# Counting image 0's key ranks by triangles, with TensorE adding the other half

## The chip, the cores and the metric

The program runs on one core of a Trainium2 chip. A core has five engines with a queue of their own: TensorE (PE; its weight loads are listed as PEld), VectorE (DVE), ScalarE (ACT), GpSimd (POOL) and SyncE (SP), which here only issues transfers. Each queue is worked off in order; engines wait for each other by semaphores. The metric is device time in microseconds (us); lower is better.

## The reference, cut to what matters

The input x has 2 images of 256 channels and 64 x 64 places, so N = 4096 places an image. Two layers follow each other.

```python
# layer 0: a sparse attention
e = prelu(batchnorm(conv3x3(x)))                 # 64 channels
sim = e^T e ; p = sparsemax(sim)                 # rows of 4096
x = x @ p + x
# layer 1: a pairwise layer with a relu of a sum
a   = w_t . theta(x)      # one number a place
bsc = w_p . phi(x)        # one number a place, the "key"
f = relu(a[n] + bsc[m] + wf_b) / N
y = f @ g(x)              # y[n] = sum over m with key[m] > -a[n] of (a[n] + key[m]) * g[m] / N
x = batchnorm(wz @ y) + x
```

Layer 1 needs no 4096 x 4096 matrix: if the places m are sorted by their key, then y[n] is taken from running sums of g[m] and key[m] * g[m] up to the position of -a[n] in the sorted keys. Sorting means that each place must learn its rank: the number of places whose key is larger, with ties broken by index.

## The kernel before, in words

Both images stay in SBUF. Layer 0 (lines 341 to 863) makes e by convolution, surveys e^T e for the few rows whose sparsemax is not just the place itself, recomputes up to 3 x 128 such rows (`rows`, 12 units of 1024 columns), and multiplies them into x (`attend`: 16 blocks an image of 3 matmuls of 128x512, each added to x by VectorE after GpSimd multiplied that stretch of x by a mask). Layer 1 starts with `project` (image 0) or `project_in` (image 1): for each tile of 128 places g, the key and a.

The class `Ranked` (lines 980 to 1257) does layer 1 by sorting. Image 0 does it with all R = 32 tiles of keys; image 1 with R = 16 tiles, while its other 16 tiles are multiplied out directly by `pair_f` (ScalarE writes relu(a + key) for 128 x 1024 pairs) and `pair_py` (TensorE, 64 steps of two matmuls). The steps for an image are:

- `keys` (line 994): the keys are made fit to be compared; `spread` sends them through DRAM and brings them back as one row in all partitions (`kb`, 128 x R*128).
- `above` (line 1027), once a tile t of 128 places: each partition compares its own key with all R*128 keys and adds the results up, as two instructions, the columns before tile t and those from it on. On VectorE it is a comparison with 0 or 1 as result (line 1041); on ScalarE a sign with -1 or 1 (line 1036), which is halved later. The comparison results go to `junk` and are not read; only the sums (`cnt`) count. The planner picks the engine of each tile.
- `ties` (line 1052): equal keys within a tile, on VectorE.
- `place` (line 1060), every 4 tiles: the sums become ranks.
- `scatter` (line 1072): GpSimd writes each tile's rows of g and keys into a DRAM table `sg` at their ranks.
- `load`, `products`, `sums`, `before`, `raised`, `stored` (lines 1086 to 1122): the sorted table is read back, summed up, and stored as `tb`. `load` needs all scatters of its image. For image 0 it overwrites the place of `kb` and of `ga_0`.
- `segments`, `places`, `counts` (1132 to 1157): find for each a its position; `fetch` (1159): GpSimd gathers the rows of `tb`; `taken` and `finish` (948, 1169): scale, turn, multiply by wz, add to x, send out.

All instructions are put on their queues by a planner (`Plan`, line 94). Each task has a cost for every engine that can do it, a rank (smaller goes first among tasks that are not late), tasks that it comes after, and `Ring` holds that stand for the buffers of a pool (`ring_sim` for the 3 PSUM tiles of `ps_sim`). The planner takes the tasks by its own estimates of time, so that a change of costs, ranks or tasks moves instructions on every queue. The ranks are the constants of line 281 (`A1` for image 1's attention, `K0` and `K1` for the counts, `PY` for the pair products and so on).

Two lines of `begin` (1215 and 1219) make the counts of an image:

```python
u = plan.task({"D": 0.25 + 0.00107 * n, "A": 0.66 + 0.00083 * n}, lambda e, t=t: self.above(t, e == "A"), r, [sp, *room])
places += [u, plan.task({"D": 0.36}, lambda t=t: self.ties(t), r + 0.02, [sp, *room])]
```

Of the kernel before, what the change touches and what calls it, by code (L numbers as in the profile page):

```python
# [8 lines left out]
F32 = mybir.dt.float32  # L9
# [10 lines left out]
P = 128  # L20
# [170 lines left out]
def sparse_path(ctx: ExitStack, tc, a, out, rows_i):  # L191
# [89 lines left out]
    DB, CV1, LS, RW0, SV1, RW1, A0, G0, A1, R0, K0, CH0, R1, K1, CH1, P1, P2, SP1, PY, PF = -16.17, 6.58, -12.34, -22.91, -12.37, -25.58, 4.52, -11.7, -8.57, -12.21, -3.49, 3.38, 7.24, 3.51, 6.34, -23.46, 1.78, 11.05, 19.06, -27.14  # L281
# [698 lines left out]
    class Ranked:  # L980
# [8 lines left out]
        def __init__(self, b, ga, R, at):  # L989
            self.b, self.ga, self.R, self.at, self.junk = b, ga, R, at, None  # L990
            self.key = None if ga is None else ga[:, 0:R, CI + 1]
            self.on_act = []
# [34 lines left out]
        def above(self, t, on_act):  # L1027

            self.made()
            kb, cnt = self.kb, self.cnt  # L1030
            n = self.R * P
            for d, (c0, c1) in enumerate(((0, t * P), (t * P, n))):
                if c0 == c1:
                    continue
                if on_act:
                    nc.scalar.activation(  # L1036
                        self.junk[:, 0, c0:c1], kb[:, c0:c1], AF.Sign, scale=STEEP,
                        bias=self.bound[:, d, t : t + 1], accum_out=cnt[:, t, 3 + d : 4 + d],
                    )
                else:  # L1040
                    nc.vector.tensor_scalar(  # L1041
                        self.junk[:, 1, c0:c1], kb[:, c0:c1], self.key[:, t : t + 1], None,
                        (ALU.is_ge, ALU.is_gt)[d], ALU.add, accum_out=cnt[:, t, d : d + 1],
# [4 lines left out]
        def made(self):  # L1048
            if self.junk is None:
                self.junk = self.at("junk", [P, 2, self.R * P], BF16)  # L1050

        def ties(self, t):

            self.made()
            nc.vector.scalar_tensor_tensor(  # L1055
                self.junk[:, 1, ts(t, P)], self.kb[:, ts(t, P)], self.key[:, t : t + 1], low,
# [3 lines left out]
        def place(self, t0):  # L1060

            b = self.b
            for t in range(t0, t0 + 4):
                if t in self.on_act:
                    nc.vector.memset(self.cnt[:, t, 0:1], float(self.R * P // 2))
# [3 lines left out]
            nc.vector.tensor_reduce(rk[:, 1], cnt[:, :, 3:5], AX.X, ALU.add)  # L1069
            nc.vector.scalar_tensor_tensor(self.rank[:, ds(t0, 4)], rk[:, 1], 0.5, rk[:, 0], ALU.mult, ALU.add)  # L1070
# [133 lines left out]
        def begin(self, rank, after, ranked, chained, then, room):  # L1204
# [7 lines left out]
            self.places_done, self.ranked, places = [], [], []  # L1212
            for t in range(self.R):
# [654 lines left out]
```

## Time and profile before

| | us |
|---|---|
| median of 3 runs | 702.23 (701.17 to 708.35) |
| the profiled execution | 735.76 |
| its span, first to last instruction | 734.0 |
| TensorE busy | 610.9 |
| VectorE busy | 538.9 |
| ScalarE busy | 380.4 |
| GpSimd busy | 209.0 |
| counts on ScalarE, line 1036 | 96.8 in 52 instructions |
| counts on VectorE, line 1041 | 75.5 in 42 instructions |
| scatters, line 1076 | 47.2 in 48 instructions |
| pair products, line 1437 | 127.5 in 256 records |

All durations come from one profiled execution, which took longer than the median of the others; the place of a step is given in us from the start of its span. A float32 matmul appears as two records, so that 256 records of line 1437 are 128 matmuls. A row of the timeline gives the start, the duration, the engine, the line, the operation, the tiles written and read, and in brackets how long the engine was idle before and what ended that.

### The profile page before, as it was taken

How to read it: one execution, taken by the hardware profiler on the slowest of the kernel's cores; microseconds unless marked ns; L12 is line 12 of the kernel's file. 1: busy time of each engine (PE TensorE's matmuls, PEld its weight loads, DVE VectorE, ACT ScalarE, POOL GpSimd, SP SyncE). 2: the span in 40 equal slices, each digit the busy share in tenths (PEclk: the TensorE clock that was granted, in tenths of full speed). 3: DMA queues.
4: the chain of work that ended last, by engine and by line, in shares of the span. 5: the costliest groups of instructions: out<-in, count | busy, mean ns of one | idle time of the engine just before them, and what ended most of it. 6: DMA issues, size and time to landing. Idle time of an engine off the chain costs nothing.

```text
span 734.0 us, 7973 instructions
## 1 busy us (share of the span) xinstructions
PE 610.9 (83%) x2629; PEld 295.4 (40%) x2629; DVE 538.9 (73%) x1052; ACT 380.4 (52%) x534; POOL 209.0 (28%) x274
## 2 busy tenths in 40 slices
PE   5998999999778699999895767759979986971993
PEld 4664444444332233434542223554445543430441
DVE  6876877877879878677759999977988835661404
ACT  0123575666458474764047999979934411400340
POOL 0118920000030311102020675440520176175300
PEclk9998999999889899999988888969989767997898
DMA  9621000101210000000113000127133534474304
GB/s 350 202 58 30 1 15 15 29 1 29 87 28 0 1 0 1 0 1 1 58 28 145 7 29 18 34 87 207 37 90 101 240 104 131 174 235 129 108 1 149
DMA packets 32824, 54.42 MB, mean 74 GB/s; under 512 B 12786, under 2 KB 19812, under 8 KB 31876
## 3 DMA queue, kind: packets, MB, share of 16 engines
q1 hardware_dynamic: 27252, 40.60, 16.5%
q0 software_dynamic: 5088, 12.61, 6.3%
q10 hardware_dynamic: 432, 0.59, 0.3%
q8 instruction: 23, 0.38, 0.2%
q14 instruction: 29, 0.24, 0.1%
HBM read 31.62 MB, written 20.07 MB: 70 GB/s over the span
## 4 chain that ended last, share of the span: by engine, by line
PE 54%; DVE 25%; issue 6%; DMA 5%; another core or an unknown queue 4%; ACT 3%; POOL 2%; SPq 0%; DVEq 0%; ACTq 0%; POOLq 0%
PE sv L476 15%; PE av L836 8%; DVE junk L1041 8%; PE py L1437 7%; PE cv_out L363 6%; PE cv_in L363 6%; PE g L873 2%; DVE junk L1055 2%; PE pz L960 2%; DMA kb<-rd_k 2%; PE sv L508 2%; PE pk L1145 2%; DVE mq L777 2%; POOL r L1162 2%
## 5 line engine op out<-in xcount | busy, mean ns | idle before, releaser
L528 ACT ACTIVATE sv<-sv,nthr 128x1024 f32<-128x1024 f32 (+1 forms) x133 | 131.2, 986 | 96.7 <-PE sv L508 48.9
L524 DVE TENSOR_TENSOR xbs<-sv,xbs 128x1024 f32<-128x1024 f32 (+1 forms) x120 | 130.7, 1089 | 38.4 <-PE sv L476 31.3
L476 PE MATMUL sv<-e 64*128 64x512 f32 x512 | 135.4, 641 | 2.3 <-DVE lim L534 1.2
L836 PE MATMUL av<-z,xbs 128*128 128x512 f32 x192 | 106.9, 693 | 30.2 <-DVE x L843 16.1
L1437 PE MATMUL py<-f,ga 128*128 128x512 f32 x256 | 127.5, 649 | 0.0
L1429 ACT ACTIVATE f<-ab,ga 128x1024 f32<-128x1024 f32 x64 | 71.6, 1142 | 103.9 <-issue 59.9
L1036 ACT ACTIVATE junk<-kb,bound 128x1536 bf16<-128x1536 f32 (+26 forms) x52 | 96.8, 1861 | 5.8 <-DMA kb<-rd_k 5.2
L1162 POOL DMA_INDIRECT r<-tb,k x64 | 61.6, 962 | 81.4 <-DVE tab L1109 38.4
L1041 DVE TENSOR_SCALAR_CACHE_REDUCE junk<-kb,ga 128x1664 bf16<-128x1664 f32 (+20 forms) x42 | 75.5, 1834 | 2.6 <-DMA kb<-rd_k 2.1
L836 PEld LDWEIGHTS av<-z,xbs 128*128 128x128 f32 x192 | 38.1, 215 | 94.3 <-issue 61.7
L476 PEld LDWEIGHTS sv<-e 64*128 64x128 f32 x512 | 45.7, 195 | 68.6 <-issue 43.7
L1437 PEld LDWEIGHTS py<-f,ga 128*128 128x128 f32 x256 | 51.3, 209 | 54.1 <-issue 52.3
L1076 POOL DMA_INDIRECT sg<-ga,rank x48 | 47.2, 984 | 70.1 <-DVE rank L1070 52.1
L964 DVE SCALAR_TENSOR_TENSOR x<-pz,s,x 128x512 f32<-128x512 f32 x32 | 23.0, 746 | 60.1 <-PE pz L960 28.6
L363 PE MATMUL cv_out<-v,wu 128*64 128x256 f32 (+1 forms) x384 | 49.6, 398 | 7.5 <-DVE v L325 7.5
L363 PE MATMUL cv_in<-v,wu 128*64 128x256 f32 (+1 forms) x384 | 46.6, 382 | 1.0 <-ACT c L374 1.0
L446 POOL TENSOR_TENSOR sq<-es 128x512 f32<-128x512 f32 x8 | 8.9, 1106 | 134.3 <-ACT es L437 111.9
L363 PEld LDWEIGHTS cv_out<-v,wu 128*64 128x64 f32 x384 | 28.9, 142 | 31.5 <-issue 14.2
L1182 PE MATMUL yr<-ident,r 128*128 128x128 f32 x64 | 14.0, 307 | 29.9 <-DVE r L1175 16.1
L960 PE MATMUL pz<-yT,wz_sb 128*128 128x512 f32 x64 | 33.5, 664 | 4.7 <-DVE yT L1189 2.1
L363 PEld LDWEIGHTS cv_in<-v,wu 128*64 128x64 f32 x384 | 27.9, 136 | 21.6 <-issue 10.1
L831 POOL TENSOR_TENSOR x<-x,mask 128x1024 f32<-128x1024 f32 x16 | 34.4, 2153 | 0.0
(207 smaller groups left out, 749.4 us busy)
## 6 DMA issues: line engine op xcount, KB each, us to landing
out<-x SPq DMA_DIRECT2D x32, 256.0 KB
tb<-tab SPq DMA_DIRECT2D x3, 2056.0 KB
x<-in_x SPq DMA_DIRECT2D x8, 512.0 KB
tab<-sg SPq DMA_DIRECT2D x3, 1040.0 KB
x<-in_x SPq DMA_DIRECT2D x4, 544.0 KB
e<-e SPq DMA_DIRECT2D x16, 128.0 KB
et<-es SPq DMA_DIRECT2D x16, 128.0 KB
mask<-kd SPq DMA_DIRECT2D x2, 1024.0 KB
```

What stands on the lines that cost most here:

```text
L363: nc.tensor.matmul(d[jp, g][ts(h, CR), n, (r0 - r) * HH : (r1 - r) * HH], lhsT=taps(j, kc, dy), rhs=v[:, kc, r0 + dy - 1 : r1 + dy - 1], s ...
L476: nc.tensor.matmul(ps[:, ts(h, CB)], lhsT=lhs(h), rhs=e[ts(h, CR), q], start=True, stop=True)
L524: nc.vector.tensor_tensor(out=acc[:, cols], in0=d[i, q][:, cols], in1=acc[:, cols], op=ALU.max)
L528: nc.scalar.activation(ps, ps, AF.Relu, bias=both["nthr"][:, i : i + 1], accum_out=got_s["over"][:, i, q : q + 1])
L836: nc.tensor.matmul(pss[j, ct], lhsT=got["xb"][:, k, ts(ct, P)], rhs=got["zs"][k][:, ts(j, CB)], start=(k == 0), stop=(k == KB - 1),)
L960: nc.tensor.matmul(d["z"][:, ct], lhsT=wz_sb[:, ts(ct, P)], rhs=d["y"], start=True, stop=True)
L1036: nc.scalar.activation(self.junk[:, 0, c0:c1], kb[:, c0:c1], AF.Sign, scale=STEEP, bias=self.bound[:, d, t : t + 1], accum_out=cnt[:, t, 3 ...
L1041: nc.vector.tensor_scalar(self.junk[:, 1, c0:c1], kb[:, c0:c1], self.key[:, t : t + 1], None, (ALU.is_ge, ALU.is_gt)[d], ALU.add, accum_ou ...
L1076: rows = nc.gpsimd.indirect_dma_start(out=self.sg, out_offset=bass.IndirectOffsetOnAxis(ap=self.rank[:, t : t + 1], axis=0), in_=self.ga[: ...
L1162: nc.gpsimd.indirect_dma_start(out=self.r[:, t % TH], out_offset=None, in_=self.tb, in_offset=bass.IndirectOffsetOnAxis(ap=self.k[:, t : t ...
L1429: nc.scalar.activation(fm, am, AF.Relu, bias=bm)
L1437: nc.tensor.matmul(pys[q][:, ts(h, CB)], lhsT=ga1[0][:, m, 0:CI], rhs=f[0][:, m % 4, ts(h, CB)], start=(m == NR), stop=(m == NT - 1),)
```

## The change

For image 0 (R = NT = 32, `folded`), `above` compares tile t only with the columns from tile t on. The results are 0 or 1 (VectorE) or -1 or 1 (ScalarE), kept as bf16 in one of four slots (two tiles, `junk` in room S3 and `junk2` in S5, two halves each). For every later tile u, the column sums of what tile t wrote tell how many of t's keys are smaller than each key of u; 128 minus that is what u would have counted against t. `below` adds these column sums up on TensorE: stationary is a column of ones (or of halves for a tile from ScalarE), moving are up to 512 columns of the slot, and the result is one row of PSUM, at partition 0, 32, 64 or 96, and in bank 0 or 1, for each 512 keys. The sums stay in one `ps_sim` tile; a product with zeros opens and closes each bank. After tile 14 the first 16 tiles' sums are complete, after tile 30 the others'. Then `below_out` copies each row of 512 to SBUF, `below_turned` turns it into columns by four matmuls with a stationary row and -1, and `place` adds it, with the known constant, to the tile's own count. So image 0 is placed after tile 15 and after tile 31, not every 4 tiles. Image 1 (R = 16) counts as before. `ties` writes to a tile of its own. Image 0's counts also come after the last products of image 1's `rows`, whose e lies in S5, and `pair_rest`, which writes to S5, comes after the counts. The planner's ranks on line 281 are changed, and a rank BE for the new tasks is added.

```diff
-    DB, CV1, LS, RW0, SV1, RW1, A0, G0, A1, R0, K0, CH0, R1, K1, CH1, P1, P2, SP1, PY, PF = -16.17, 6.58, -12.34, -22.91, -12.37, -25.58, 4.52, -11.7, -8.57, -12.21, -3.49, 3.38, 7.24, 3.51, 6.34, -23.46, 1.78, 11.05, 19.06, -27.14
+    DB, CV1, LS, RW0, SV1, RW1, A0, G0, A1, R0, K0, CH0, R1, K1, CH1, P1, P2, SP1, PY, PF, BE = 6.71, 6.58, -12.34, -12.34, -12.37, -12.64, -10.46, -11.7, -4.84, -15.38, 3.21, 3.33, -11.7, 3.51, 6.41, 4.08, -11.87, -6.07, 12.61, -11.87, -4.72
...
+            self.slots, self.ring, self.folded = [], Ring(4 if R == NT else 2), R == NT
...
+        def slot(self, i):
+            if not self.slots:
+                for name in ("junk", "junk2")[: self.ring.n // 2]:
+                    junk = self.at(name, [P, 2, self.R * P], BF16)
+                    self.slots += [junk[:, 0], junk[:, 1]]
+            return self.slots[i % self.ring.n]
+
+        def above(self, t, on_act, d):
+            slot = d["slot"] = self.slot(self.used if self.folded else int(on_act))
+            self.used += 1
+            kb, cnt, n = self.kb, self.cnt, self.R * P
+            d["on_act"] = on_act
+            for k, (c0, c1) in enumerate(((0, t * P), (t * P, n))):
+                if c0 == c1 or (self.folded and k == 0):
                     continue
...
+        def below(self, t, d):
+            def zeros(h, **flags):
+                nc.tensor.matmul(
+                    self.sums_of[:, h], lhsT=part_ones[:, 2:3].to_broadcast((P, P)), rhs=d["slot"][:, N - CB : N], **flags
+                )
+            if t == 0:
+                self.sums_of = ps_sim.tile([P, CT, CB], F32, name=f"below_{self.b}", tag="sim")
+                for h in range(CT):
+                    zeros(h, start=True, stop=False)
+            for q in range((t + 1) // 4, self.R // 4):
+                c0, c1 = max((t + 1) * P, q * CB), (q + 1) * CB
+                p = 32 * (q % 4)
+                nc.tensor.matmul(
+                    self.sums_of[p : p + 1, q // 4, c0 - q * CB : CB], lhsT=part_ones[:, ds(int(d["on_act"]), 1)],
+                    rhs=d["slot"][:, c0:c1], start=False, stop=False,
+                )
+            if t % 16 == 14:
+                zeros(t // 16, start=False, stop=True)
+
+        def below_out(self, q, d, e):
+            p = 32 * (q % 4)
+            row = d["row"] = work.tile([P, CB], F32, name=f"below_{self.b}_{q}", tag="wa")
+            (nc.scalar.copy if e == "A" else nc.vector.tensor_copy)(row[p : p + 1], self.sums_of[p : p + 1, q // 4])
+
+        def below_turned(self, q, d):
+            p = 32 * (q % 4)
+            d["bt"] = ps_av.tile([P, 4], F32, name=f"bt_{self.b}_{q}", tag="av")
+            for k in range(4):
+                nc.tensor.matmul(
+                    d["bt"][:, k : k + 1], lhsT=d["row"][p : p + 1, ts(k, P)], rhs=minus[p : p + 1, 0:1],
+                    start=True, stop=True,
+                )
...
+        def place(self, t0, bt):
...
+                if self.folded:
+                    known = t * P - sum(u in self.on_act for u in range(t)) * (P // 2)
+                    known += (R - t) * P // 2 if t in self.on_act else 0
...
+                if not last:
+                    v = plan.task(
+                        {"P": 0.15 + 0.1 * (self.R // 4 - (t + 1) // 4)}, lambda t=t, d=d: self.below(t, d), BE, [u] + below[:1],
+                        take=None if t else hb, free=[hj],
+                    )
...
+                if t % 16 == 14:
+                    for q in range(q - 3, q + 1):
+                        hr, ho, d = ring_y.hold(), ring_av.hold(), {}
+                        waiting.append((q, d, ho))
+                        v = plan.task(
+                            {"D": 0.6, "A": 0.65}, lambda e, q=q, d=d: self.below_out(q, d, e), ranked - 0.7, list(below),
+                            take=hr, free=[hb] if 4 * q + 4 == self.R else [],
+                        )
+                        self.ranked.append(v)
+                        d["turned"] = plan.task({"P": 0.6}, lambda q=q, d=d: self.below_turned(q, d), BE, [v], take=ho, free=[hr])
+                if t % 16 == 15:
+                    for q, d, ho in waiting:
+                        placed(q, places[q] + [d["turned"]], d, [ho])
...
-        {"kb": "S0", "tab0": "S0", "tab1": "S6", "r": "S0", "junk": "S3"},
+        {"kb": "S0", "tab0": "S0", "tab1": "S6", "r": "S0", "junk": "S3", "junk2": "S5"},
...
-    r0.begin(R0, [turn0], K0, CH0, {"ab": a_of_0, "rest": None}, conv1)
+    r0.begin(R0, [turn0], K0, CH0, {"ab": a_of_0, "rest": None}, [*conv1, *rw1])
...
-        rest_tasks.append(plan.task({"A": 0.95}, lambda q=q: pair_rest(q), PF - 1, [u], free=[hq]))
+        rest_tasks.append(plan.task({"A": 0.95}, lambda q=q: pair_rest(q), PF - 1, [u, *r0.ranked], free=[hq]))
```

## The prediction

> **What bounds the kernel now.** I read the granted clock and span first (734.0 us in the span, 735.76 us for the execution, clock 0.906), then the chain that ended last, then busy time by stretches of 20 us, then the timeline of each engine from 370 us on. TensorE is the busiest engine, and VectorE's counting lines head what is left of the chain. The stretches show where:
>
> ```profile
> PE 610.9 (83%) x2629; PEld 295.4 (40%) x2629; DVE 538.9 (73%) x1052; ACT 380.4 (52%) x534; POOL 209.0 (28%) x274
> ...
> 420.00:440.00 20.00, 13.13 (x26) 5.24 (x25) 19.82 (x36) 19.84 (x21) 14.76 (x23) 0.83 0.10 33
> 440.00:460.00 20.00, 15.57 (x32) 6.54 (x31) 18.58 (x34) 19.84 (x19) 10.19 (x16) 0.83 0.06 20
> ...
> 500.00:520.00 20.00, 19.22 (x46) 8.67 (x47) 18.17 (x47) 20.00 (x27) 4.21 (x8) 1.00 0.53 142
> ```
>
> In a row the columns are the stretch, then the busy time of PE, PEld, DVE, ACT and POOL. From 400 to 490 us VectorE and ScalarE are full, and TensorE idles a third: this is image 0's count, into which image 1's attention is woven. From 500 us on TensorE is full too. The landmarks I measure by, from the timelines:
>
> ```profile
> 399.40 3.71 ACT L1036 ACTIVATE junk<-kb,bound 128x4096 bf16<-128x4096 f32 x1 [3.97 <-DMA kb<-rd_k]
> 404.15 0.39 ACT L1036 ACTIVATE junk<-kb,bound 128x128 bf16<-128x128 f32 x1
> 404.53 3.59 ACT L1036 ACTIVATE junk<-kb,bound 128x3968 bf16<-128x3968 f32 x1
> ...
> 402.90 0.48 DVE L1041 TENSOR_SCALAR_CACHE_REDUCE junk<-kb,ga 128x256 bf16<-128x256 f32 x1
> 403.30 4.21 DVE L1041 TENSOR_SCALAR_CACHE_REDUCE junk<-kb,ga 128x3840 bf16<-128x3840 f32 x1
> ...
> 464.46 8.23 PE L899 MATMUL g<-gw_sb,x 128*128 128x131 f32 x72
> 489.72 0.39 PE L924 MATMUL pt_k<-ident,ga 128*16 128x128 f32 x1 [4.75 <-DVE bound L1008]
> 494.76 1.88 PE L1437 MATMUL py<-f,ga 128*128 128x512 f32 x4
> ...
> 492.53 0.97 POOL L1076 DMA_INDIRECT sg<-ga,rank  x1 [0.22 <-issue]
> 498.09 2.60 SPq L1091 DMA_DIRECT2D tab<-sg  x2
> 535.48 0.48 DVE L1136 TENSOR_SCALAR oh<-ab,lims 128x512 f32<-128x512 f32 x1
> 583.85 0.98 POOL L1162 DMA_INDIRECT r<-tb,k  x1 [38.42 <-DVE tab L1109]
> ```
>
> So image 0's last scatter starts at 492.5, its table is loaded from 498.1, image 1's keys are turned at 489.7, the pair products (py) start at 494.8, image 0's segments at 535.5, and the fetches at 583.9. After 599 us the records hold two gaps with no visible releaser:
>
> ```profile
> 599.26 11.52 another core or an unknown queue
> 663.48 14.65 another core or an unknown queue
> ```
>
> They make 26 of the 33 us by which this execution exceeds the median of 702.23. I treat them as not part of the ordinary runs, make the sum against the profiled execution as differences, and carry the difference over to the median.
>
> **What the Trainium skill says.** "TensorEngine Tiling (Array Packing)", Key Properties: column tiles work independently, so weight loads and matmuls of different tiles run in parallel, and changing the tiling mode drains the array. The trace agrees on the first: convolution matmuls on two 64-column tiles have a mean record of 382 to 399 ns, yet 24 records take 2.74 us in the chain, 114 ns each. "TensorE: Matmul & The Clock Gate", Back-to-back issue gap: one bf16 matmul of 512 columns takes about 216 ns warm and 427 cold. No such matmul is in this trace; its float32 ones, two records each, take 0.86 us warm (py, 3.45 us for 8 records). "SBUF — State Buffer", Who interferes with whom: a VectorE instruction with two SBUF inputs is held off by a GpSimd instruction that reads SBUF. The trace agrees: the tie instruction (L1055), 0.35 us alone, took 1.66, 1.91 and 2.21 us beside the mask products (2.15 us).
>
> **The change, part by part.**
>
> *Removed.* Image 0's 32 counts of 4096 columns become counts of 128 to 4096, 67,584 columns in place of 131,072. From start to start, ScalarE's cost is 0.33 us + 0.84 ns a column and VectorE's 0.13 us + 1.04 ns (from the five rows above). A full tile cost 4.09 us in its two parts on ScalarE and 4.53 on VectorE. In the built order ScalarE keeps 20 tiles with 44,800 columns, 6.6 + 37.6 = 44 us for about 82; VectorE 12 tiles with 22,784, 1.6 + 23.7 = 25 us for 54. That frees 38 and 29 us in a stretch that both engines fill. It is not what the end gains, because of what follows.
>
> *Added on TensorE.* 136 row sums (8 a tile for tiles 0 to 2, 7 for the next four, down to one), 4 zero products and 32 products of one column. The sums cycle over four 32-column tiles. If all four overlap, the bound is about 0.05 us each; warm in series it is 0.22, cold in series 0.43. I take 0.12: like the convolution's pairs. The upper end costs 93 x 0.31 = 29 us where it counts, see below. Below nothing is excluded: nothing is removed from TensorE.
>
> *A wait added.* There are four junk slots, and a count can start only when TensorE has summed the tile four before it. TensorE's queue is in order, and the built order is: first attention blocks among sums 0 to 5, then nine attention blocks in a row (1_2_0 to 1_6_0), then sum 6. So the counters run four tiles ahead and stop. Estimate: count 0 starts at 395.4 (ScalarE's copy of the key row stands earlier in its queue, before the copies that held it until 390.6); sum 5 is done at about 416; nine blocks x 3 x 0.87 us end at 439.5. ScalarE ends tile 9 at about 419 and then idles 20 us. Queued behind the waiting count is nothing but further counts, but VectorE's place, which image 0's scatters wait for, is behind them. From 439.5: 84 sums x 0.12 = 10, nine attention matmuls 7.8, 16 one-column products 1.5, and 3 of waits on the counters, which run one tile ahead: the first projection (g) at 462, beside 464.5 now. The other half of the freed time goes here.
>
> *Then it pays.* Now VectorE is behind with counts until 488, so projections stand half finished and the keys are late. After: four projection groups x 3.1 us, 9 sums, 16 one-column products and waits, 16 us, and the keys of image 1 are turned at 478.4, 11.3 us earlier. Its key row lands at about 486.5 (8.1 us later, as now), and py starts at about 479, 15 us earlier (ring of the product PSUM: one of three tiles is held by the sums until then; two are enough for the projections, since each is read out within 1 us).
>
> *Moved on GpSimd.* Tiles are now ranked in two batches of 16. The first rank needs count 15, sum 14, a row copy (0.6) and a turn: about 454.5. Then 32 scatters x 1.27 us = 41 us without a pause, so the last ends at 495.3, where it is 493.5 now: scatters started at 418.4 and were spread under the counting. SyncE's table load goes from 498.1 to about 500; behind it in SyncE's queue wait the last key row and image 1's last block of a, needed late. So image 0's table is not earlier. What moves is the work that VectorE had before it: count 1 starts 11 us earlier, so segments start at about 521 (535.5 now). A count tile and six ties (5 us) now lie inside the segments and sums, which leaves the raised table 10 us earlier (557 for 567.3), and the fetches start at about 573.5.
>
> *Small terms.* Row copies (8 x 0.6), the extra memsets and the ties' own tile cost under 5 us on VectorE, inside its slack of 416 to 440. The new rest-after-counts wait is met 30 us before its use. Before 377 us both kernels issue nearly the same order; I take zero.
>
> **Sum.** The fetch path moves by -10, the TensorE path by -15. In the ordinary runs, without the two gaps, TensorE is nearly full from 494 on (about 188 us busy to 724), so its start counts for more than the fetch path: -12 us. The profiled execution would be near 724, the median 702.2 - 12 = **690 us**.
>
> **Rivals.** (1) *Scatters bind* (chance 0.24): the table arrives at 500 to 503, the products wait there 6 us on VectorE with counts queued behind, and the fetch path gains only 3 to 5 us: 698. For it: 41 us of scatters after a first rank at 454; against: TensorE has py to fill in. (2) *Sums in series* (0.12): they don't overlap, and clock gaps while TensorE waits for counters make them cold (granted clock was 0.50 to 0.59 just after idle in this stretch). From 0.25 us a sum, 93 x 0.13 = 12 us, the gain is gone; at 0.43 the counters, ranks and scatters end 29 us later and the time is 719, slower. Against: the convolution's overlap. (3) *The stall is shorter* (0.20): the attention blocks run faster, ranks start near 445, and both paths move by 20: 682. My forecast of 685 to 695 has 0.44. That the sums don't do what they say is no rival: each comparison not made is implied by one made.
>
> **Numbers.** The range is 679 to 704: it takes in rivals 1 and 3, and of rival 2 the part under 0.27 us a sum. Within 1%, 695.2 to 709.3, is about what a measurement can't tell from no change. Faster 0.64 (forecast and rival 3), same 0.24 (rival 1), slower 0.12 (rival 2).
>
> **What would show it.** Right: ScalarE idle about 20 us between counts 9 and 10; g at about 462; keys turned near 478; py near 479; first scatter near 454 and scatters without a pause to 495; table load at 500; segments near 521; a sum every 0.1 to 0.15 us. Wrong: a sum every 0.25 us or more; no idle time in the counts; a scatter end after 500; or a TensorE that idles over 20 us after 500 because f or the fetches come late.

## The result

Beside each other on one chip, the kernel before takes 703.28 us and the kernel after 699.66 us (medians of 20 runs each); the ratio is 0.9936, with an interval of 0.9914 to 0.9957. A second comparison gave 703.47 and 698.48 us, with the same ratio (0.991 to 0.9962). So the change gains 3.6 to 5.0 us. The forecast was 12.

The profiled execution of the kernel after took 699.12 us, with a span of 697.4. Its page and its busy time by stretches, for the rows shown of the kernel before:

```profile
PE 619.3 (89%) x2833; PEld 297.5 (43%) x2833; DVE 523.8 (75%) x1047; ACT 344.5 (49%) x502; POOL 210.8 (30%) x274
...
420.00:440.00 20.00, 16.64 (x38) 6.47 (x36) 19.39 (x53) 0.00 (x0) 6.80 (x7) 1.00 0.00 1
440.00:460.00 20.00, 19.23 (x107) 7.90 (x108) 17.05 (x28) 13.07 (x13) 2.27 (x3) 1.00 0.00 0
500.00:520.00 20.00, 19.94 (x44) 8.79 (x45) 18.06 (x53) 19.31 (x30) 6.75 (x11) 0.91 0.65 179
```

The order of the columns is that of the prediction's rows. ScalarE (the fourth busy column), full from 400 to 490 us in the kernel before, does nothing at all from 420 to 440. VectorE has as much to do as it had, although it counts far less. The wait behind this and the landmarks, from the list of waits and the timelines:

```profile
ACT junk L1051 <- PE below L1079: 37.5, 5, 27.3
```

```profile
392.98 3.75 ACT L1051 ACTIVATE junk<-kb,bound 128x4096 bf16<-128x4096 f32 x1
...
446.93 2.64 ACT L1051 ACTIVATE junk<-kb,bound 128x2816 bf16<-128x2816 f32 x1 [27.28 <-PE below L1079]
...
460.02 1.07 POOL L1136 DMA_INDIRECT sg<-ga,rank  x1 [17.75 <-DVE rank L1127]
...
469.61 2.96 PE L899 MATMUL g<-gw_sb,x 128*128 128x131 f32 x24
...
488.65 0.27 PE L924 MATMUL pt_k<-ident,ga 128*16 128x128 f32 x1
...
488.86 1.88 PE L1535 MATMUL py<-f,ga 128*128 128x512 f32 x4
...
496.90 2.00 ACT L1051 ACTIVATE junk<-kb,bound 128x2048 bf16<-128x2048 f32 x1 [2.79 <-DMA kb<-rd_k]
...
503.08 2.41 SPq L1151 DMA_DIRECT2D tab<-sg  x2
...
524.75 0.48 DVE L1196 TENSOR_SCALAR oh<-ab,lims 128x512 f32<-128x512 f32 x1
...
576.05 1.03 POOL L1222 DMA_INDIRECT r<-tb,k  x1 [34.19 <-DVE kf L1216]
```

Image 0's counts start at 393.0 (395.4 was forecast), ScalarE waits 27.3 us for a row sum (20), the first scatter starts at 460.0 (454.5), the first projection of image 1 at 469.6 (462), image 1's keys are turned at 488.65 (478.4), py starts at 488.9 (479), image 1's key row has landed at 496.9, when its first count starts (486.5), the table is loaded from 503.1 (500), the segments start at 524.75 (521) and the fetches at 576.05 (573.5). Image 0's table, segments and fetches came 3 to 4 us later than forecast. What concerns image 1 came 8 to 10 us late.

The profile of before that the prediction shows stems from an execution of 735.76 us. A clean one (703.56 us, span 701.8) is used from here on; its first projection of image 1, py, first count of image 1 and segments:

```profile
462.73 8.23 PE L899 MATMUL g<-gw_sb,x 128*128 128x131 f32 x72
493.03 1.88 PE L1437 MATMUL py<-f,ga 128*128 128x512 f32 x4
497.57 2.00 ACT L1036 ACTIVATE junk<-kb,bound 128x2048 bf16<-128x2048 f32 x1 [2.73 <-DMA kb<-rd_k]
535.17 0.48 DVE L1136 TENSOR_SCALAR oh<-ab,lims 128x512 f32<-128x512 f32 x1
```

### The profile page after: what moved, and what is told of

It reads as the page before. It is cut to its first block, busy times and chain, and to the rows that moved or that the text cites. A ratio compares the mean times of both kernels' runs of the same rounds, so it can differ in the third digit from the quotient of the medians.

```text
span 697.4 us, 8373 instructions
## 1 busy us (share of the span) xinstructions
PE 619.3 (89%) x2833; PEld 297.5 (43%) x2833; DVE 523.8 (75%) x1047; ACT 344.5 (49%) x502; POOL 210.8 (30%) x274
## 4 chain that ended last, share of the span: by engine, by line
PE 55%; DVE 28%; DMA 7%; issue 5%; POOL 3%; ACT 1%; SPq 0%; DVEq 0%; ACTq 0%; POOLq 0%
PE sv L476 16%; PE av L836 8%; PE cv_out L363 6%; PE cv_in L363 6%; PE py L1535 5%; DVE junk L1056 4%; DVE mq L777 4%; DMA r<-tb,k 3%; DVE tied L1104 3%; PE pz L960 2%; PE g L873 2%; DVE xbs L524 2%; DVE tab L1176 2%; PE sv L508 2%; DVE tab L1169 2%
## 5 line engine op out<-in xcount | busy, mean ns | idle before, releaser
L524 DVE TENSOR_TENSOR xbs<-sv,xbs 128x1024 f32<-128x1024 f32 (+1 forms) x120 | 130.7, 1089 | 37.6 <-PE sv L476 30.5
L1535 PE MATMUL py<-f,ga 128*128 128x512 f32 x256 | 119.0, 613 | 0.0
L836 PE MATMUL av<-z,xbs 128*128 128x512 f32 x192 | 104.4, 671 | 9.8 <-DVE x L843 5.0
L1051 ACT ACTIVATE junk<-kb,bound 128x1792 bf16<-128x1792 f32 (+22 forms) x35 | 60.9, 1747 | 40.3 <-PE below L1079 37.5
L1535 PEld LDWEIGHTS py<-f,ga 128*128 128x128 f32 x256 | 48.5, 197 | 50.7 <-issue 49.3
L836 PEld LDWEIGHTS av<-z,xbs 128*128 128x128 f32 x192 | 35.9, 207 | 69.8 <-issue 46.9
L1056 DVE TENSOR_SCALAR_CACHE_REDUCE junk<-kb,ga 128x1280 bf16<-128x1280 f32 (+17 forms) x28 | 45.9, 1665 | 4.3 <-DMA kb<-rd_k 2.4
L363 PEld LDWEIGHTS cv_in<-v,wu 128*64 128x64 f32 x384 | 27.9, 136 | 21.6 <-issue 10.1
L1235 DVE SCALAR_TENSOR_TENSOR r<-r,a 128x128 f32<-128x128 f32 x64 | 20.7, 348 | 20.3 <-DMA r<-tb,k 20.1
L533 DVE MAX8 top<-sv 128x8 f32<-128x1024 f32 x27 | 33.0, 1223 | 0.0
```

Source lines behind the costliest of these rows:

```text
L363: nc.tensor.matmul(d[jp, g][ts(h, CR), n, (r0 - r) * HH : (r1 - r) * HH], lhsT=taps(j, kc, dy), rhs=v[:, kc, r0 + dy - 1 : r1 + dy - 1], s ...
L524: nc.vector.tensor_tensor(out=acc[:, cols], in0=d[i, q][:, cols], in1=acc[:, cols], op=ALU.max)
L836: nc.tensor.matmul(pss[j, ct], lhsT=got["xb"][:, k, ts(ct, P)], rhs=got["zs"][k][:, ts(j, CB)], start=(k == 0), stop=(k == KB - 1),)
L1051: nc.scalar.activation(slot[:, c0:c1], kb[:, c0:c1], AF.Sign, scale=STEEP, bias=self.bound[:, k, t : t + 1], accum_out=cnt[:, t, 3 + k : 4 ...
L1056: nc.vector.tensor_scalar(slot[:, c0:c1], kb[:, c0:c1], self.key[:, t : t + 1], None, (ALU.is_ge, ALU.is_gt)[k], ALU.add, accum_out=cnt[:, ...
L1535: nc.tensor.matmul(pys[q][:, ts(h, CB)], lhsT=ga1[0][:, m, 0:CI], rhs=f[0][:, m % 4, ts(h, CB)], start=(m == NR), stop=(m == NT - 1),)
```

## The experiments

Three explanations were set against each other. **A**: VectorE's queue, where ties are held up by GpSimd's mask products, delays image 1's attention, and through it the keys of image 1. **B**: the scatters and image 0's table bind, rival 1 of the forecast. **Rival 2**: the row sums are dear. Two more came up on the way: **C**, about the first group of runs, and **D**, SyncE's queue.

The table gathers what the runs on a 703 us chip showed. "Key row" is the start of the first count of image 1 (what waits for that row's landing), "table" the issue of image 0's table load, both in us of the profiled execution, as are "fetch", the first fetch, and the span. The runs of the table were made in three groups, in which the kernel before took 703.47 us (after, ranks_only, early_ranks), 702.52 (folded_only, ties_gated, early_keys_first) and 703.91 (the last three rows); each ratio is to the kernel before of its own group, so across groups the ratios are the better comparison. A median is of 4 runs (ranks_only) to 20. A profiled execution can lie off its median: that of ties_gated was the fastest of its six runs (692.79 us), that of early_keys_first the slowest (693.05 us).

| kernel | median | ratio to before (95%) | key row | table | fetch | span |
|---|---|---|---|---|---|---|
| before | 703.47 | | 497.6 | 497.9 | 584.5 | 701.8 |
| after | 698.48 | 0.9936 (0.9910 to 0.9962) | 496.4 | 502.6 | 577.0 | 696.2 |
| ranks_only | 710.91 | 1.0123 (1.0046 to 1.0201) | 510.1 | 490.0 | 582.4 | 707.2 |
| folded_only | 702.42 | 0.9997 (0.9973 to 1.0021) | 500.9 | 517.5 | 581.0 | 699.1 |
| ties_gated | 695.07 | 0.9896 (0.9869 to 0.9924) | 490.8 | 496.0 | 574.0 | 691.1 |
| early_ranks | 700.82 | 0.9962 (0.9945 to 0.9980) | 503.2 | 488.7 | 580.5 | 699.0 |
| early_keys_first | 690.07 | 0.9819 (0.9790 to 0.9848) | 492.1 | 492.8 | 569.4 | 691.2 |
| combined | 697.76 | 0.9906 (0.9873 to 0.9939) | 496.3 | 492.4 | 574.2 | 696.0 |
| sums_twice_b | 704.56 | 1.0013 (0.9994 to 1.0032) | 501.0 | 507.8 | 583.2 | 702.5 |
| sums_sooner_b | 710.05 | 1.0089 (1.0061 to 1.0117) | 510.7 | 495.5 | 589.5 | 708.6 |

### The first group of runs

These four ran in one group in which the kernel before took 735.8 us, so they are compared with that, and with each other up to 447 us, where they run as elsewhere.

The kernel before, unedited:

> The kernel before, unedited, for a profiled execution without the two unexplained gaps of 11.5 and 14.7 us. Every theory: 703 us, span about 701, with the landmarks of the first profile up to 599 us within 3 us (first projection g 464, keys of image 1 turned 490, table load 498, segments 535, fetches from 584), and after that no gap over 5 us without a releaser. If the gaps come back, they belong to the kernel and the forecast's base was wrong.

It took 735.99 us (ratio 1.0001). The two gaps of the prediction's profile came back, 12.1 us at 599.6 and 14.4 us at 666.6. So they are not chance events of one execution. They don't belong to the kernel as such either, as the expectation had it: they are missing in the clean profile (before_third, below). They go with the runs of about 735 us.

The ties left out:

```diff
- lambda t=t: self.ties(t), r + 0.02
+ lambda t=t: None if self.folded else self.ties(t), r + 0.02
```

> The kernel after, with the 32 tie instructions of image 0 left out (their slots in the order stay empty; the counts of equal keys of lower number are missing from the ranks). Theory A (VectorE's queue, with ties held up about 1.9 us each by GpSimd's mask products, delays the attention): about ten ties of 2.24 us and twenty of 0.35 us go, the nine attention blocks end near 440 where they ended at 446, the idle time of ScalarE falls from 27 to about 21 us, and the end comes 4 to 6 us earlier: 694 to 696. Theory B (the masks themselves, not VectorE's queue, pace the attention): attention ends at 445 to 446 and the end is within 2 us of 699.7.

Of theory A the first half is met:

```profile
414.47 23.44 PE L836 MATMUL av<-z,xbs 128*128 128x512 f32 x54
437.84 1.89 PE L1079 MATMUL below<-junk,part_ones 128*1 128x128 bf16 x25
```

TensorE does the nine attention blocks (54 records) without a pause in 23.44 us, the forecast's 9 x 3 x 0.87; in the kernel after they take 28.8 us. ScalarE's idle time was 21.0 us, ending at 438.5 where it is 446.9 after, and the first projection started at 462.1 in place of 469.6. (The "theory B" of this expectation, that the mask products themselves set the pace of the attention, is refuted by the same lines; it is not the B above.) The time was 738.72 us, 0.4% above before, and says nothing on the end: the key row landed at 511.7 because of a standstill, shown at the end of this document.

Two more kernels: in sums_twice each sum is made twice, the second time with zero weights; in sums_sooner the attention's rank is -4.80 in place of -4.84:

> The kernel after with each of the 136 row sums followed by the same product with zero weights (values unchanged). Theory A (sums cost 0.07 us each and are no part of the missing gain): 136 x 0.07 = 9.5 us more on TensorE, of which two thirds lie after the stall; first projection 5 to 6 us later, end 702 to 706. Rival 2 of the forecast (sums in series, 0.25 us or more): at least 93 x 0.25 = 23 us, end above 718. If TensorE has slack there: 699 to 701.

> The kernel after with the rank of image 1's attention raised from -4.84 to -4.80, so that five attention blocks stand between sum 5 and sum 6 in TensorE's queue in place of nine; order elsewhere nearly the same. Theory A: idle time of ScalarE falls by four blocks (10 us) from 27 to about 17, first scatter at about 449 (459.6 after), table load at about 492 (503), while the attention ends 1 to 2 us later. If the scatters and the table set the end (rival 1): 692 to 695. If TensorE's own work, started by the end of attention, sets it: 699 to 702.

They took 754.83 and 755.65 us. Neither says anything on its theories, since standstills of 5 to 9 us lie in both between 453 and 505; both were run again, below.

### After and before on one chip

> The kernel after, unedited, beside the kernel before on one chip. The four runs before this one fell on a chip on which the kernel before takes 735.8 us, and where engines stand still with no visible releaser while GpSimd issues indirect DMAs one after the other. Theory C (the change makes such a train of 32 scatters where there were groups of four, so that chip charges it twice): on a chip where before takes 736, after takes 735 to 745, with one standstill of 8 to 12 us of VectorE between 490 and 506 that before doesn't have; on a chip where before takes 703, after takes 699 to 700 again. If the standstills have nothing to do with the train: the ratio is 0.99 on either.

> The kernel before, unedited, for a profile from the same chip as the other kernels of this call. Where it takes 703 us, no gap without a releaser in its chain and the fetches of 64 rows without a pause over 3 us; where it takes 736, the two gaps of 12 and 14 us again at about 600 and 667.

In this group the kernel before took 703.47 us. After took 698.48 us, and no wait of more than 2.2 us without a releaser is in either profile. Theory C wasn't tested by it: the kernel after never ran in a group with 736 us.

### The two halves of the change

The ranks of the change in the kernel before; then the change with the old ranks (the sums' rank kept):

> The kernel before with only the line of ranks of the kernel after (19 of 20 values differ), comparisons as before: the other part of the change alone. If the gain comes from fewer comparisons: 702 to 710 (ratio 1.00 to 1.01). If it comes from the new ranks (attention of image 1 ahead of the counts): 696 to 700 (0.99 to 0.995).

> The kernel after with the 20 rank values of the kernel before (the rank of the sums, -4.72, kept): the comparisons are halved, but TensorE's queue is ordered by the old ranks: attention of image 1 stands ahead, 33 blocks before the sums of tile 6, so that the counters stop earlier and longer. Theory A (the stall of the counters behind the attention is what eats the gain): ScalarE idle for 30 us or more, ranks and table later than after by 5 to 10 us, end 700 to 708 (ratio 0.995 to 1.007). If the gain is the halved counting alone, whatever the order: 696 to 700.

The new ranks alone cost 7.4 us (four runs; the interval is 3 to 14), the halved comparisons alone gain nothing that can be told, and both together gain 5.0. So the halved counting is worth some 12 us under the new ranks, and of the two cases that were expected for ranks_only the first was nearer: the gain comes from fewer comparisons. In folded_only ScalarE was idle for 40 us behind sums, the time is inside what theory A expected, and the table came 15 us later than after, more than the 5 to 10 expected; still the loss against after is 4 us, much less than the table's. The key row, 4.5 us later than after, and the first fetch, 4.0, fit that loss.

### What delays the attention

Theory A's step is the held-up tie. The timelines of GpSimd and VectorE in the kernel after:

```profile
423.08 2.12 POOL L831 TENSOR_TENSOR x<-x,mask 128x1024 f32<-128x1024 f32 x1
423.11 2.24 DVE L1104 SCALAR_TENSOR_TENSOR tied<-kb,ga,low 128x128 bf16<-128x128 f32 x1
...
426.29 2.12 POOL L831 TENSOR_TENSOR x<-x,mask 128x1024 f32<-128x1024 f32 x1
426.32 2.24 DVE L1104 SCALAR_TENSOR_TENSOR tied<-kb,ga,low 128x128 bf16<-128x128 f32 x1
...
430.34 0.34 DVE L1104 SCALAR_TENSOR_TENSOR tied<-kb,ga,low 128x128 bf16<-128x128 f32 x1
```

A tie takes 0.34 us alone. One that starts just after a mask product ends with it, 2.24 us later; four of these lie between 423 and 443 us, 4 x 1.9 = 7.6 us, each ahead of an addition of the attention that frees a PSUM tile for TensorE and lets the next mask product start. The Trainium skill ("SBUF — State Buffer", Who interferes with whom) says that a VectorE instruction with two SBUF inputs contends with a GpSimd instruction that reads SBUF; a tie reads `kb` and `low` from SBUF, and the trace agrees. TensorE's nine blocks in the same kernel, between sum 5 and sum 6:

```profile
417.54 8.16 PE L836 MATMUL av<-z,xbs 128*128 128x512 f32 x18 [0.84 <-DVE x L843]
426.07 2.84 PE L836 MATMUL av<-z,xbs 128*128 128x512 f32 x6 [0.37 <-DVE x L843]
430.48 7.99 PE L836 MATMUL av<-z,xbs 128*128 128x512 f32 x18 [1.56 <-DVE x L843]
439.90 2.84 PE L836 MATMUL av<-z,xbs 128*128 128x512 f32 x6 [1.44 <-DVE x L843]
443.51 2.84 PE L836 MATMUL av<-z,xbs 128*128 128x512 f32 x6 [0.77 <-DVE x L843]
```

Its waits for additions sum to 5.0 us. It is the held-up ties that make them, and not the ties' own time: from 430.3 to 434.7 VectorE does ten ties that aren't held up, five ahead of each addition, and TensorE does three blocks without a wait. In the kernel before ties were held up too, but there TensorE waited for additions that stood behind whole counts, up to 4.9 us at a time.

Taken away by starting the ties later, with all the work kept (the second edit chains the sums one after another):

```diff
- lambda t=t: self.ties(t), r + 0.02, [sp, *room])
+ lambda t=t: self.ties(t), r + 0.02, [sp, *room, *(self.masked if folded else [])])
...
- BE, [u] + below[:1],
+ BE, [u] + below[-1:],
...
+ r0.masked = [last1[6, 1]]
```

> The kernel after, all work kept, with image 0's 32 ties started only when block 1_6_1 of the attention has been added (GpSimd's mask products are over then), and the row sums chained one after another. On a chip where before takes 703.5. Theory A (ties held up by the mask products delay the attention): nine attention blocks end at 438 to 440 (446 after), ScalarE's idle time 20 to 21 us (27), first projection 3 to 6 us earlier than 469.5, since the ties now take 11 us of VectorE behind the attention; key row of image 1 and py 2 to 5 us earlier, end 694 to 697. If these 7 us are hidden by the scatters, the table and SyncE's queue: 698 to 700, like after.

```profile
427.72 0.75 DVE L843 SCALAR_TENSOR_TENSOR x<-av,b,x 128x512 f32<-128x512 f32 x1 [1.82 <-PE av L836]
...
435.97 2.64 ACT L1051 ACTIVATE junk<-kb,bound 128x2816 bf16<-128x2816 f32 x1 [21.61 <-PE below L1079]
...
452.48 2.96 PE L899 MATMUL g<-gw_sb,x 128*128 128x131 f32 x24
469.10 5.61 PE L899 MATMUL g<-gw_sb,x 128*128 128x131 f32 x24
```

Now VectorE waits for TensorE at each addition, as the forecast had assumed; ScalarE's idle time is 21.6 us, ending 11 us earlier, the first projection starts 17 us earlier, and the key row lands 5.6 us earlier than after. The time is 695.07 us, 3.4 us less than after (2.8 by the ratios, just clear of the noise), inside what theory A expected. Of the 17 us, 11 are the earlier end of the idle time; the rest is order, since the planner now has the first projection ahead of sums that it follows in the kernel after. By the second projection only 4 of the 17 us are left: the sums that were to be done before now stand between the two, the ties stand on VectorE among the last counts, TensorE waits for these one by one, 4.9 us in all, and the second group of 24 records, which takes 2.96 us in the kernel after, takes 5.61. The granted clock of 457 to 480 us is 0.63 here and 0.85 after.

### Whether the counters' stall, the sums or the table set the end

The attention's rank -4.80, so that five blocks stand ahead of sum 6 and not nine:

> The kernel after with the rank of image 1's attention raised from -4.84 to -4.80, so that five attention blocks stand between sum 5 and sum 6 in place of nine, on a chip where before takes 703. If the counters' idle time (27 us) as such is what eats the gain: it falls to 16 to 18 us, first scatter near 452, and the end is 692 to 695. Theory A (the stall trades one for one with the attention, which TensorE then does later): first projection 1 to 3 us later than 469.5, end 698 to 701.

The idle time fell to 14.3 us and the first scatter came 7 us earlier, as expected, and so did the table (495.5). The time was 710.05 us, 11.6 us more than after (10.8 by the ratios): worse than every theory had it. Seven blocks of the attention, three in the kernel after, now stand among sums whose counts come one at a time, so the first projection started at 482.6 (469.4 after). On SyncE's queue the table then stands ahead of the key row, which was written at 497.2:

```profile
495.54 2.64 SPq L1151 DMA_DIRECT2D tab<-sg  x2
498.24 2.33 SPq L1154 DMA_DIRECT2D nxt<-sg  x1
500.61 3.49 SPq L1021 DMA_DIRECT2D tb<-zero  x1
504.21 0.31 SPq L932 DMA_DIRECT2D rd_k<-row_k  x1
```

So the key row landed 14 us later than after, some 8 us of it from the late keys and 6 from SyncE's queue. An idle time that is halved and a table that is 7 us earlier went along with 11.6 us lost. Neither sets the end here.

> The kernel after with each of the 136 row sums followed by the same product with zero weights (values unchanged), for the price of a sum on the end, on a chip where before takes 703. Theory A (0.07 us a sum in pieces of six to nine): 9.5 us more on TensorE, of which the part behind the stall, 93 sums, delays ranks and projections by 6 to 7 us; end 703 to 706. Rival 2 of the forecast (0.25 us a sum or more): 23 us or more, above 718. If TensorE's time before 470 is hidden by other waits: 699 to 701.

704.56 us, 6.1 us more than after (5.4 by the ratios), where theory A expected 703 to 706: 0.04 us for each of the 136 sums that were added. Their own time is seen in the timeline of the kernel after, 25 records in 1.89 us, 0.076 us each:

```profile
446.29 1.89 PE L1079 MATMUL below<-junk,part_ones 128*1 128x128 bf16 x25
```

Rival 2 is refuted. If the first set of sums costs what the second does, they take 5 to 6 us of the end; the forecast had 10 us for them in TensorE's queue.

### Ranks as they come, and SyncE's queue

Each quarter of a row-sum bank is closed and read when its own tiles are summed:

```diff
- if t % 16 == 14:
-     zeros(t // 16, start=False, stop=True)
+ if t % 4 == 2:
+     q = t // 4
+     p = 32 * (q % 4)
+     nc.tensor.matmul(self.sums_of[p : p + 32, q // 4], lhsT=part_ones[:, 2:3].to_broadcast((P, 32)),
+                      rhs=d["slot"][:, N - CB : N], start=False, stop=True)
...
- if t % 16 == 14:
-     for q in range(q - 3, q + 1):
+ if t % 4 == 2:
...
- if t % 16 == 15:
+ if t % 4 == 3:
```

> The kernel after, with each quarter of a row-sum bank closed and read as soon as its own tiles are summed, so that image 0's tiles are ranked four at a time (8 ranks) as they come and not in two batches of 16. Work is the same but for 8 closing products of 32 columns in place of two of 128. If scatters and table bind (rival 1): first scatter at about 449 in place of 460, last at 488 to 492 in place of 500, table load 8 to 12 us earlier, and the end 4 to 8 us earlier than after: 692 to 696 (ratio to before 0.984 to 0.990). If TensorE's own work binds: within 2 us of after.

The first scatter came at 446.7, the table at 488.65, 14 us earlier than after, more than expected, and the keys were turned 6.4 us earlier. The time was 700.82 us, 2.3 us more than after. Theory B falls here: with scatters and table well ahead, the end doesn't come earlier. SyncE's and ScalarE's timelines show where the 6.4 us of the keys went:

```profile
484.56 0.24 ACT L928 COPY row_k<-pt_k 16x128 f32<-16x128 f32 x1
488.65 2.71 SPq L1156 DMA_DIRECT2D tab<-sg  x2
491.41 2.47 SPq L1159 DMA_DIRECT2D nxt<-sg  x1
493.98 3.25 SPq L932 DMA_DIRECT2D rd_k<-row_k  x1
```

The key row is written at 484.8 and its store starts at 494.0. It stands in line behind a zero row, which waits for GpSimd's queue of scatters until 487.5, and behind the table that the earlier ranks had brought forward. Two edits change that order:

```diff
- nc.gpsimd.memset(zero, 0.0)
+ nc.vector.memset(zero, 0.0)
...
- ld = plan.task({"S": 0.1}, self.load, rk, self.places_done, lat=8.45)
+ ld = plan.task({"S": 0.1}, self.load, rk, self.places_done + self.behind, lat=8.45)
...
+ keys1 = plan.gate()
+ r0.behind = [keys1]
...
+ plan.let_go(keys1, [r1.spread])
```

> The kernel that ranks four tiles at a time (700.8), with two edits on SyncE's queue: image 0's table is loaded behind image 1's key row and not ahead of it, and the zero of image 1's table is written by VectorE, so that its store doesn't wait for GpSimd's scatters. In that kernel the key row was ready at 484.8 and its store started at 494.0, behind the zero row and the table, and TensorE waited 14.1 us for the a row. Theory D (SyncE's order eats what earlier ranks give): key row landed at 491 to 493 (503), wait of 14 us on TensorE down to under 3, end of the pair products at 670 to 674 (682), end 688 to 692. If the fetches' train binds instead: fetches start within 3 us of 580 and the end stays at 698 to 701.

```profile
485.49 0.24 ACT L928 COPY row_k<-pt_k 16x128 f32<-16x128 f32 x1
485.76 0.33 SPq L932 DMA_DIRECT2D rd_k<-row_k  x1
...
492.76 2.51 SPq L1156 DMA_DIRECT2D tab<-sg  x2
```

690.07 us: 10.8 us less than early_ranks (10 by the ratios) and 8.4 less than after, inside theory D's numbers. The table is loaded 4 us **later** than in early_ranks, the key row lands 11.1 us earlier, and the first fetch, which is of image 0, comes 11.2 us earlier: in VectorE's queue the first counts of image 1, which wait for the key row, stand ahead of the products of image 0's table. The wait of 14.1 us that the expectation names fell to 1.6. In early_ranks it was this:

```profile
508.61 0.38 PE L924 MATMUL pt_a<-ident,ga 128*8 128x128 f32 x1 [14.11 <-DVE ga L906]
```

The line is the turn that makes the a row; it waits for `ga` on VectorE, which stands there behind the first count of image 1, and so behind the key row. TensorE's queue has the same order in both kernels. On VectorE the planner also moved this `ga` ahead of the products of image 0's table, which gives about 2 of the 12.5 us; the rest is the key row. This is the best kernel of the study, 1.8% below before.

The two remedies together, ties behind block 1_6_0:

> Three edits together: ranks four tiles at a time, image 1's key row ahead of image 0's table on SyncE's queue (690.1 with these two), and image 0's ties behind the attention block 1_6_0 with the sums chained (695.1 alone, 3.4 less than after). If the gains add: attention ends near 453, scatters at 446 to 485, end 685 to 688. If the scatters (32 in a row at 1.27 us) and the fetches (64 at 1.26 us) bind by then: 689 to 692, no gain over the two edits.

697.76 us: they don't add, and the second spoils the first. The attention did end at 457, 12 us earlier than after, but TensorE then waited for counts and row copies, which the ties stood among (clock 0.71 in 457 to 480), and the second projection came late:

```profile
457.46 2.96 PE L899 MATMUL g<-gw_sb,x 128*128 128x131 f32 x24
...
474.84 5.53 PE L899 MATMUL g<-gw_sb,x 128*128 128x131 f32 x24
```

The key row landed at 496.3, as in the kernel after, and the time is that of the kernel after within 1 us (2 by the ratios), although image 0's table is loaded 10 us earlier.

**What the table says.** In all nine kernels with new ranks or folded counts, the span ends 196 to 202 us after the key row of image 1 has landed (before: 204), while it ends 182 to 217 us after the table's load. The first fetch is nearly as steady a mark, 117 to 125 us before the end. Two pairs speak for the key row: combined and after have the same key row and the same span, with fetches 2.8 us apart; ties_gated and early_keys_first have the same span, with key rows 1.3 and fetches 4.6 us apart. A likely way from the key row to the end is image 1's own table, which needs image 1's counts: its load is issued 150 to 156 us before the end in all ten kernels, before included. That way wasn't tested by itself. early_ranks against early_keys_first is the only direct edit of the key row's place, and it moved the fetches with it; the other kernels only agree.

## Why the prediction was off

It had the direction, the stall and its cause; the gain was less than half of the forecast's. Its way of adding up roughly fits what was measured: the fetches moved by -7.5 us and the start of py by -4.4, and the end by -3.6 to -5.0. What was wrong is the size of the two moves, -10 and -15 in the forecast. Point by point:

- **Removed.** Right. The counting line of ScalarE fell from 96.8 to 60.9 us and that of VectorE from 75.5 to 45.9 (both images), 36 and 30 us for the 38 and 29 forecast. (The forecast's rows give ScalarE a fixed cost of 0.27 us and not 0.33, 1 us in the sum.)
- **Added on TensorE.** 0.076 us a sum where 0.12 was taken. The mistake was in the gain's favour.
- **The wait added.** The mechanism is as forecast, ScalarE stops after tile 9 and idles until sum 6, but the end of the nine attention blocks, put at 439.5, was 446.3. **This is the step that failed**, and its root is the line of the small terms. It has row copies, memsets and "the ties' own tile" at under 5 us on VectorE, "inside its slack of 416 to 440", and puts the ties themselves at nothing. There was no slack: VectorE was busy for 19.4 of the 20 us from 420 to 440. Seven ties of image 0 ran beside mask products at 1.9 to 2.2 us each, four of them in the stretch of the nine blocks, 7.6 us ahead of additions, for which TensorE waited 5.0 us. The forecast had quoted the very rule and its 2.21 us, and then left it out of the sum. With the ties left out (ties_off) the nine blocks take the 23.4 us of the forecast, and with the ties out of the way (ties_gated, ties_off) the idle time is 21 to 22 us, against the 20 forecast.
- **Then it pays.** The first projection was to come 2.5 us earlier than before; it came 6.7 later (469.4 for 462.7). From it to the keys 19 us were needed in place of 16.4, the key row took 7.9 to 8.2 us more (8.1). So of the 10 us by which the key row was late against the forecast, 7 are the attention's end. The key row was to land 11 us earlier than before; it landed 1.2 earlier. For py, 4.4 us earlier came of the 15. Putting the ties right doesn't give all of it back: ties_gated is 2.8 to 3.4 us faster than after, of the 7 to 8 that were missing.
- **Moved on GpSimd.** Scatters without a pause, first at 460.0, table at 503.1: 3 to 6 us late, again from the attention's end. Segments came 11 us earlier than before (the forecast: 14.5) and fetches 7.5 (10), but not for the reason given, that count 1 starts 11 us earlier: it started 1.2 us earlier. From the first count of image 1 to the segments VectorE took 27.9 us; the forecast had 34.5, and before it is 37.6. In the new order seven of image 1's 16 count tiles stand on VectorE ahead of the segments where ten stood before, and ScalarE has eight of the 16 where it had six. So a row that was 10 us late and a stretch that was 7 us short nearly cancelled, and that the segments came near the forecast is luck. This part gives the gain: from the key row's landing to the end 4.4 us less than before, and 1.2 from the row itself, 5.6 us in the two profiles, 5.0 in the medians.
- **The base.** Leaving out the two gaps was right for these runs: in the clean profile of before neither exists, and its span (701.8) fits the median.
- **Rivals.** Rival 1 named 698 and a table at 500 to 503, and both numbers came (the median within 2 us), but its mechanism only in small part. VectorE's products waited 1.3 us for the table where rival 1 had 6, and in the kernel before 1.1. The line is from after_again:

```profile
512.61 0.17 DVE L1161 COPY kr<-tab 128x16 f32<-128x16 f32 x1 [1.29 <-DMA tab<-sg]
```

Kernels with the table 7 and 14 us earlier were slower, but in these the table also went ahead of the key row; combined, with the table 10 us earlier and the key row in its place, ended with the kernel after. The wait also says that on VectorE the table is the later of the two by 1.3 us, so that an earlier key row alone would lengthen it; the two kernels that gained, ties_gated and early_keys_first, have both the key row and the table earlier than after. Rival 2 is refuted by sums_twice_b. Rival 3 didn't occur; ties_gated comes nearest to it, with the first scatter at 451.1, and its time is 695, not 682, because the counts then come late. The likeliest case had the key row of image 1 in its working, at 486.5, but only as the start of VectorE's counts; the runs point to it as what the end follows, and SyncE's queue, in which it can stand behind the table, had no price in the forecast.

## What to carry to other kernels

When freed time is to reach the end, follow the one transfer that the next stage waits for (here a key row of 16 x 128 numbers) through every queue that it passes, SyncE's included: some 10 us were gained by letting it go ahead of a table that was needed later. A short instruction that can be held up by another engine must be priced at its held-up time wherever it stands in an in-order queue ahead of work on the path. A landmark that comes near its forecast doesn't show that the reason was right: look at what stands before it. Engine time that is idle proves nothing: with the counters' idle time halved the kernel was 11 us slower, since TensorE then waited for counts one at a time and the key row stood behind the table on SyncE's queue.

## What the runs showed of the hardware

**Standstills in the first group.** In the four kernels of the group where before takes 736 us, engines stood still with no visible releaser while GpSimd issued scatters or fetches one after the other. In ties_off:

```profile
501.90 0.97 POOL L1136 DMA_INDIRECT sg<-ga,rank  x1 [0.21 <-issue]
505.54 0.98 DVE L910 TENSOR_TENSOR ga<-g,gb_sb 128x786 f32<-128x786 f32 x1 [11.07 <-remote]
505.61 0.26 ACT L928 COPY row_k<-pt_k 16x128 f32<-16x128 f32 x1 [13.19 <-issue]
```

The last scatter starts at 501.9. ScalarE's operand, the turned keys, was there from 493.1; it and VectorE go on at 505.5, and TensorE, which had issued single products at intervals of 1 to 2 us, is back at its pace at 505.4. The same shape stands at 600 and 667 us in the kernel before, where GpSimd fetches. In the other groups no such wait of more than 2.2 us is in any profile, with the same trains of scatters and fetches. What starves the engines there wasn't settled. The number of the chip doesn't tell it: this group and the last one, in which the kernel before took 703.9 us, are both listed under chip 2. The kernel after wasn't measured where before takes 736 us: whether it is faster there is open.

**A slow clock in some groups of the projection.** 24 records of the projection take 2.96 us at a granted clock of 1.00, and 5.53 and 5.61 us, at 0.52 and 0.50, in the kernels in which TensorE had just waited for counts one at a time (combined and ties_gated). That the waits bring the clock down wasn't tested: in the kernel after a group of 24 that follows one-column products took 4.62 us at 0.64, with no wait over 0.5 us just before. A slow group costs 1.7 to 2.6 us here, a small part of what ties_gated lost of its lead.
